# A 3x3 convolution of image rows in blocks of four from six (six products in place of twelve), inside a kernel with attention and dynamic filters

## The chip, the cores and the metric

One core of one Trainium2 chip. The time is device microseconds (us) of one execution, the median of several. "Ratio" is the mean time of one kernel's fast runs over the mean of the other kernel's fast runs in the same rounds, with a 95% interval; it is therefore not quite the ratio of the medians quoted beside it. Runs of different calls are compared through their ratios to the kernel before, which ran again in each call (medians 3262.8 to 3268.4 us).

Engines: PE is TensorE's matrix multiplication, PEld its weight load, DVE VectorE, ACT ScalarE, POOL GpSimd, SP the queue that issues most transfers.

## The reference, cut to what matters

```python
# x: 4 images, 256 channels, 48 x 48, fp32
x = x + layer0(group_norm(x))   # conv 3x3, batch norm, relu, qkv 1x1, attention (8 heads), projection
x = x + layer1(group_norm(x))   # below

def layer1(x):
    guidance = conv3x3(x, W_cat)                     # 45 maps = 5 dilations x 9 taps
    outs = [x]
    for i, d in enumerate((1, 6, 12, 24, 36)):
        w = softmax(guidance[:, 9*i:9*(i+1)], axis=1)
        outs.append(sum of 9 shifted copies of x, each times one map of w)   # "dynamic filter"
    y = conv1x1(concat(outs), W_scale)               # 1536 -> 256 channels, "the mix"
    return batch_norm_with_batch_statistics(y)       # over all four images
```

## The kernel before: the parts that matter

Image 0's convolution runs alone. Then attention of image b alternates with a *mixed stage*, in which the dynamic filters of image b and the convolution and qkv of image b+1 share the engines. There are three mixed stages, then a last filter stage without a convolution, then a tail that reloads, normalizes and stores everything.

```python
# the convolution: 6 row blocks x 2 output halves x 18 matmuls of 384 columns an image, straight from the padded image
nc.tensor.matmul(pc[:, :CH], wc[:, i, k, o * P : (o + 1) * P],
                 window(gn, i, c * R, k // 3 - 1, k % 3 - 1), ...)
...                                    # ScalarE: relu(scale * pc + bias) -> hid
# one tap of a dynamic filter
nc.tensor.matmul(pw[:, : nr * WW], pick[:, k : k + 1].to_broadcast([2 * NG, P]), w[...])  # "wb": a map on 128 partitions
nc.vector.tensor_tensor(pv, wb, src, ALU.mult)        # "prod": PSUM x SBUF, five buffers
dst = accv[:, :, l0:l1, x0:x1]
eng = nc.vector if n in own else nc.gpsimd            # own = {1} in the last stage, else empty
eng.tensor_tensor(dst, dst, pv, ALU.add)              # "cat": four buffers
tap += 1
owed += NH * nr * ncol * rate
pump()                                                # issue the other work's matmuls for that much TensorE time
```

`pump` hands out matmuls of three queues: mixes of finished accumulators, the guidance of later rows, and the next image's convolution and qkv. So the convolution is filler for TensorE between the taps. The filter's two sides are: TensorE (wb) to VectorE (prod) to GpSimd (add) to TensorE (mix).

## Time and profile before

| | before |
|---|---|
| time, median | 3268.6 us |
| first convolution matmul; start of attention of image 0 | 19.95; 209.2 us |
| mixed stage 2: lead-in, filter stretch | 64.7, 293.5 us |
| GpSimd busy in that stretch | 258.8 us (88%) |
| tail: from the last copy of a result out of PSUM to the end | 42.8 us |

Read it by stage, not by totals. The *lead-in* of a mixed stage is from attention's end to GpSimd's first add, the *filter stretch* from there to its last add. The prediction shows these rows for the first mixed stage. The second one is the same to 0.1 us. Columns: stretch, its length, then busy time (instructions) of PE, PEld, DVE, ACT and POOL, the granted TensorE clock, the DMA engines' share and GB/s.

```profile
1374.30:1439.00 64.70, 64.70 (x248) 34.92 (x246) 14.47 (x31) 5.83 (x10) 0.00 (x0) 0.97 0.05 13
1439.00:1732.50 293.50, 293.50 (x1102) 184.15 (x1101) 198.24 (x287) 33.24 (x56) 258.78 (x192) 1.00 0.05 14
```

TensorE is full in both; GpSimd is close behind in the second.

### The profile page before, as it was taken

Reading aid. Unit: us, or ns where it says so; the run is one execution under the profiler, and the core shown is the slowest. Engines: PE = TensorE matmul, PEld = TensorE weight load, DVE = VectorE, ACT = ScalarE, POOL = GpSimd, SP = SyncE. Lnnn points to the kernel's source line nnn. Section 1 sums busy time; section 2 is a strip of 40 time slices with the busy share of each in tenths; the row PEclk is TensorE's granted clock in tenths of the full one; section 3 lists DMA queues with packets and bytes.
Section 4 is the critical chain, followed back from the end, with each engine's and each line's share of the span. In section 5 each row is a group of like instructions: output and inputs, shape, how many; then the busy total and the mean of one; then the engine's idle time right before and its main releaser. Section 6 shows DMA issues by size and latency. Waiting matters only on the chain.

```text
span 3262.5 us, 43612 instructions
## 1 busy us (share of the span) xinstructions
PE 3099.3 (95%) x18070; PEld 1390.5 (43%) x18070; DVE 2272.3 (70%) x2149; ACT 1491.8 (46%) x1673; POOL 973.3 (30%) x746
## 2 busy tenths in 40 slices
PE   7999999999999999999999999999999999978883
PEld 4542223555662222456664222355565222234442
DVE  2048888556668888736676888836666898867776
ACT  0058887400028887600026887820013888740002
POOL 0000000069870000038982000008885000006663
PEclk9999999999999999999999999999999999988876
DMA  3020000000003000000003000000001000031004
GB/s 124 15 44 6 4 3 11 16 15 20 10 13 56 6 6 11 11 8 25 13 10 63 6 6 11 6 6 5 10 5 39 1 5 6 11 140 49 10 5 184
DMA packets 71245, 81.40 MB, mean 25 GB/s; under 512 B 51568, under 2 KB 62336, under 8 KB 67968
## 3 DMA queue, kind: packets, MB, share of 16 engines
q1 hardware_dynamic: 70240, 73.15, 8.0%
q0 software_dynamic: 800, 5.41, 0.4%
q8 instruction: 142, 2.33, 0.3%
q14 instruction: 63, 0.52, 0.1%
HBM read 50.23 MB, written 28.31 MB: 24 GB/s over the span
## 4 chain that ended last, share of the span: by engine, by line
PE 87%; DVE 5%; ACT 4%; issue 2%; DMA 1%; POOL 0%; SPq 0%; DVEq 0%; ACTq 0%; POOLq 0%
PE se L718 20%; PE pc L637 17%; PE num L748 17%; PE py L1008 12%; PE wb L1067 5%; PE pg L890 5%; PE pq L660 4%; PE den L770 3%; ACT p L727 3%; PE pp L819 2%; DVE acc L763 2%; PE pv L679 2%; DVE prod L1088 1%; ACT no L766 1%; POOL cat L1091 0%
## 5 line engine op out<-in xcount | busy, mean ns | idle before, releaser
L1091 POOL TENSOR_TENSOR cat<-cat,prod 128x752 f32<-128x752 f32 (+8 forms) x720 | 965.9, 1349 | 2240.4 <-DVE prod L1088 1261.4
L727 ACT ACTIVATE p<-se 128x1024 f32<-128x1024 f32 x1296 | 1259.2, 1026 | 277.5 <-PE se L718 238.3
L763 DVE TENSOR_TENSOR acc<-acc,p 128x2048 f32<-128x2048 f32 x504 | 1154.6, 2291 | 108.5 <-ACT p L727 69.6
L718 PE MATMUL se<-q,k 32*128 32x512 f32 (+1 forms) x5760 | 802.6, 592 | 11.2 <-ACT p L727 8.0
L1088 DVE TENSOR_TENSOR prod<-wb,pad 128x768 f32<-128x768 f32 (+7 forms) x768 | 558.9, 748 | 269.2 <-PE wb L1067 260.8
L748 PE MATMUL num<-p,vT 128*32 128x512 f32 (+1 forms) x5760 | 694.0, 561 | 8.8 <-ACT no L766 7.4
L637 PE MATMUL pc<-pad,wc 128*128 128x384 f32 x1728 | 611.6, 490 | 2.3 <-issue 2.3
L1067 PE MATMUL wb<-w,pick 90*128 90x384 f32 (+3 forms) x888 | 470.9, 558 | 51.7 <-DVE prod L1088 43.8
L718 PEld LDWEIGHTS se<-q,k 32*128 32x128 f32 x5760 | 291.3, 183 | 526.6 <-issue 422.2
L637 PEld LDWEIGHTS pc<-pad,wc 128*128 128x128 f32 x1728 | 322.4, 191 | 192.5 <-issue 12.7
L1008 PE MATMUL py<-cat,wsc 128*128 128x384 f32 x960 | 365.8, 514 | 0.5 <-POOL cat L1091 0.5
L748 PEld LDWEIGHTS num<-p,vT 128*32 128x32 f32 x5760 | 121.6, 108 | 486.7 <-issue 438.4
L1067 PEld LDWEIGHTS wb<-w,pick 90*128 90x128 f32 x888 | 172.3, 196 | 202.9 <-DVE prod L1088 76.0
L646 ACT ACTIVATE hid<-pc,bn_t_f,bn_s_f 128x384 f32<-128x384 f32 x48 | 32.2, 671 | 460.9 <-PE pc L637 460.9
L1008 PEld LDWEIGHTS py<-cat,wsc 128*128 128x128 f32 x960 | 189.4, 202 | 106.0 <-issue 18.5
L1082 DVE TENSOR_TENSOR cat<-wb,pad 128x768 f32<-128x768 f32 x114 | 108.5, 952 | 90.3 <-PE wb L1067 90.3
L890 PE MATMUL pg<-pad,wcat 128*45 128x384 f32 x864 | 153.5, 498 | 2.6 <-DVE pad L587 2.4
L1023 ACT COPY y<-py 128x768 f32<-128x768 f32 x24 | 19.2, 799 | 277.1 <-PE py L1008 277.1
L660 PE MATMUL pq<-hid,wqkv 128*128 128x384 f32 x384 | 135.3, 485 | 0.0
L763 DVE TENSOR_TENSOR acc<-p,p 128x2048 f32<-128x2048 f32 x36 | 82.5, 2293 | 66.1 <-ACT p L727 66.1
L670 DVE TENSOR_REDUCE qkpart<-q 128x1 f32<-128x384 f32 x48 | 26.5, 552 | 140.7 <-ACT q L667 139.1
L660 PEld LDWEIGHTS pq<-hid,wqkv 128*128 128x128 f32 x384 | 71.4, 190 | 41.2
(124 smaller groups left out, 1175.3 us busy)
## 6 DMA issues: line engine op xcount, KB each, us to landing
pad<-in_x SPq DMA_DIRECT2D x14, 1152.0 KB, 14.8
x_d<-pad SPq DMA_DIRECT2D x48, 192.0 KB, 2.5
y_d<-y SPq DMA_DIRECT2D x24, 384.0 KB, 2.7
xst<-in_x SPq DMA_DIRECT2D x36, 192.0 KB, 2.4
y<-y_d SPq DMA_DIRECT2D x3, 2304.0 KB, 19.6
out<-y SPq DMA_DIRECT2D x6, 1152.0 KB, 12.4
x<-x_d SPq DMA_DIRECT2D x2, 2304.0 KB, 24.4
x_first<-in_x SPq DMA_DIRECT2D x2, 1152.0 KB, 7.3
```

What stands on the lines that cost most here:

```text
L637: nc.tensor.matmul(pc[:, :CH], wc[:, i, k, o * P : (o + 1) * P], window(gn, i, c * R, k // 3 - 1, k % 3 - 1), start=(i == 0 and k == 0), s ...
L660: nc.tensor.matmul(pq[:, :CH], wqkv[:, i, s, g * P : (g + 1) * P], hid[:, i, cols], start=(i == 0), stop=(i == NH - 1),)
L718: nc.tensor.matmul(ss[j // 2][:, j % 2, at : at + n], k_[r, g, m * P : (m + 1) * P], q[r, g, q0 : q0 + n], start=True, stop=True,)
L727: nc.scalar.activation(p[:, 2 * pair : 2 * pair + 2, :], ss[pair], AF.Exp, scale=QS)
L748: nc.tensor.matmul(st["num"][r, at : at + n], vT[:, m, g * P + j * D : g * P + (j + 1) * D], p[:, j, at : at + n], start=(m == 0 and not s ...
L763: nc.vector.tensor_tensor(st["acc"], other, p, ALU.add)
L890: nc.tensor.matmul(pg[64 * s : 64 * s + NG, :CH], wcat[:, i, k, :], window(gn, i, (c + s) * R, k // 3 - 1, k % 3 - 1), start=(i == 0 and k ...
L1008: nc.tensor.matmul(py[c][:, o, :CH], wsc[:, n * NH + i, o * P : (o + 1) * P], rhs(i), start=(n == 0 and i == 0), stop=(last and i == NH - 1),)
L1067: nc.tensor.matmul(pw[:, : nr * WW], pick[:, k : k + 1].to_broadcast([2 * NG, P]), w[:, l0 * WW : l1 * WW], start=True, stop=True,)
L1082: nc.vector.tensor_tensor(accv, wb, src, ALU.mult)
L1088: nc.vector.tensor_tensor(pv, wb, src, ALU.mult)
L1091: eng.tensor_tensor(dst, dst, pv, ALU.add)
```

## The change

Intent: compute four output rows from six input rows (a minimal-filtering scheme along y), so that per four rows there are six products of three column taps in place of twelve: half of the multiplications. In exchange the inputs (VectorE), the weights (GpSimd and ScalarE, once, stored to DRAM and reloaded for later images) and the outputs (VectorE) are transformed on the chip.

```diff
-        wc = wpool.tile([P, NH, 9, C], F32, tag="wc", name="wc")
...                                     # (the weights now live in a pool of image 0 only)
+        def made_from(wc, pool):       # weights of product i, image 0
+            def make(i):
+                if i == 1: eng.tensor_tensor(t, w[0], w[2], ALU.add)          # eng = GpSimd, 1536 elements
+                if i in (1, 3): eng.tensor_tensor(u, t, w[1], ALU.add)
+                if i in (2, 4): eng.tensor_tensor(u, t, w[1], ALU.subtract)
...                                     # i = 3: two more and a nc.scalar.mul; i = 0, 5: nc.scalar.mul
+                nc.sync.dma_start(out=u_d[i], in_=u)
+        def inputs(stage, g):          # VectorE, three rounds, g = upper or lower half
+            if stage == 0:   4 x axpy of 300 elements; 2 x tensor_tensor of 600
+            elif stage == 1: 4 operations of 600, two SBUF inputs each
+            else:            4 operations of 600, two SBUF inputs each
+        def outputs(i, g, o, m):       # VectorE, m = the product in PSUM, 288 elements
...
+            elif i == 0:
+                result(1, d34, -2.0, d12)
+                result(2, s34, -4.0, s12)
+                tt(s12, s12, s34, ALU.subtract)
+                axpy(d12, d34, -8.0, d12)
+                result(0, m, None, s12)
...
+            for at, i in enumerate(ORDER):      # 6 products x 2 halves x 2 output blocks x 6 matmuls of 288
+                    if at == 0: inputs(0, g)
+                    if at in (1, 3): inputs((at + 1) // 2, g)
...
-            t = [last.tile(...) for j in range(2)]
+            t = [last.tile(...) for j in range(3)]     # tail: image 2's result is reloaded here
+            nc.sync.dma_start(out=t[2], in_=y_d[B - 2])
```

(Bodies shortened; the lines of `outputs` are whole.) The first four lines under `i == 0` (the "combinations") take both operands from SBUF; the fifth reads the product in PSUM.

More of the change, by code (lines that the diff above doesn't have):

```diff
@@ L523, in conv_preact_kernel @@
     y_d = tc.dram_tile([B, P, NH, N], F32, name="y_d")
+    u_d = tc.dram_tile([6, P, NH, 3, C], F32, name="u_d")
     with tc.tile_pool(name="w", bufs=1) as wpool, tc.tile_pool(
@@ L544, in conv_preact_kernel @@
         wsc = wpool.tile([P, (1 + len(DILATIONS)) * NH, C], F32, tag="wsc", name="wsc")
-        for h in range(NH):
-            nc.gpsimd.dma_start(out=wc[:, h], in_=conv_w[:, h])
-        nc.gpsimd.dma_start(out=wqkv, in_=qkv_w)
-        nc.gpsimd.dma_start(out=wp, in_=proj_w)
-        nc.gpsimd.dma_start(out=vbc, in_=v_b.rearrange("(h p) -> p h", p=P))
-        nc.gpsimd.dma_start(out=wcat, in_=cat_w)
-        nc.gpsimd.dma_start(out=wsc, in_=scale_w)
         ones = wpool.tile([P, D], F32, tag="ones", name="ones")
@@ L560, in conv_preact_kernel @@
         )
-        lgs = [wpool.tile([P, CH], F32, tag=f"lg{j}", name=f"lg{j}") for j in range(2)]
-        for lg in lgs:
-            nc.gpsimd.memset(lg, 0.0)
+        lg = wpool.tile([P, CH], F32, tag="lg", name="lg")
+        nc.gpsimd.memset(lg, 0.0)
         yst = wpool.tile([P, NH, B * NCK, 6], F32, tag="yst", name="yst")
         bn_s, bn_t = conv_norm(wpool, "f")
+        bn_s6 = wpool.tile([P, NH], F32, tag="bn_s6", name="bn_s6")
+        nc.vector.tensor_scalar(bn_s6, bn_s, -1.0 / 6.0, None, ALU.mult)
         pads = []
@@ L627, in conv_preact_kernel @@
         MM = 27.0 / 16 * CH
-        def conv_qkv(b, gn, psum_tile, q, k_, vT, after):
-            hid = keep("h", f"hid_{b}")
-            for c in range(NCK):
-                for o in range(NH):
-                    pc = psum_tile(f"pc_{b}_{c}_{o}")
-                    for i in range(NH):
-                        for k in range(9):
-                            nc.tensor.matmul(
-                                pc[:, :CH],
-                                wc[:, i, k, o * P : (o + 1) * P],
-                                window(gn, i, c * R, k // 3 - 1, k % 3 - 1),
-                                start=(i == 0 and k == 0),
-                                stop=(i == NH - 1 and k == 8),
-                            )
-                            if k < 8 or i < NH - 1:
-                                yield MM
-                    nc.scalar.activation(
-                        hid[:, o, c * CH : (c + 1) * CH], pc[:, :CH], AF.Relu,
-                        bias=bn_t[:, o : o + 1], scale=bn_s[:, o : o + 1],
-                    )
-                    yield MM
+        ORDER = (1, 2, 3, 4, 0, 5)
@@ new lines, in conv_preact_kernel, with taken_from, load @@
+        TJ = HH // 4 // 2
+        TN = TJ * WW
+        def taken_from(pool):
+            def load(i):
+                u = pool.tile([P, NH, 3, C], F32, tag="u", name=f"u_{i}")
+                nc.sync.dma_start(out=u, in_=u_d[i])
+                return u
+            return load
+        def made_from(wc, pool):
+            w = [wc[:, :, 3 * j : 3 * j + 3, :] for j in range(3)]
+            t = pool.tile([P, NH, 3, C], F32, tag="ut", name="u_t")
+            def make(i):
+                u = pool.tile([P, NH, 3, C], F32, tag="u", name=f"u_{i}")
+                eng = nc.gpsimd
+                if i == 1:
+                    eng.tensor_tensor(t, w[0], w[2], ALU.add)
+                if i == 3:
+                    eng.tensor_scalar(t, w[0], 0.25, None, ALU.mult)
+                    eng.tensor_tensor(t, t, w[2], ALU.add)
+                    nc.scalar.mul(w[1], w[1], 0.5)
+                if i in (1, 3):
+                    eng.tensor_tensor(u, t, w[1], ALU.add)
+                if i in (2, 4):
+                    eng.tensor_tensor(u, t, w[1], ALU.subtract)
+                if i == 0:
+                    nc.scalar.mul(u, w[0], -1.5)
+                if i == 5:
+                    nc.scalar.mul(u, w[2], -6.0)
+                nc.sync.dma_start(out=u_d[i], in_=u)
+                return u
+            return make
@@ new lines, in conv, with axpy, relu, result @@
+        def conv(b, gn, psum_tile, weights, pool, hid):
+            halves = [
+                act.tile([P, NH, 6, TJ, PADW], F32, tag=tag, name=f"cv_{b}_{tag}")
+                for tag in ("q", "k")
+            ]
+            held = act.tile([P, 4, 2 * NH, TN], F32, tag="v", name=f"cs_{b}")
+            S12, D12, S34, D34 = range(4)
+            place = {1: 1, 2: 2, 3: 3, 4: 4, 0: 1, 5: 2}
+            def inputs(stage, g):
+                v = [halves[g][:, :, i].rearrange("p h t w -> p h (t w)") for i in range(6)]
+                v4 = [halves[g][:, :, i] for i in range(6)]
+                d = [
+                    gn[:, :, 4 * TJ * g + r : 4 * TJ * g + r + 4 * TJ - 3 : 4, :] for r in range(6)
+                ]
+                tt, stt = nc.vector.tensor_tensor, nc.vector.scalar_tensor_tensor
+                def axpy(out, x, a, y):
+                    stt(out=out, in0=x, scalar=a, in1=y, op0=ALU.mult, op1=ALU.add)
+                if stage == 0:
+                    for h in range(NH):
+                        axpy(v4[5][:, h], d[2][:, h], -4.0, d[4][:, h])
+                        axpy(v4[0][:, h], d[1][:, h], -4.0, d[3][:, h])
+                    tt(v[1], v[5], v[0], ALU.add)
+                    tt(v[2], v[5], v[0], ALU.subtract)
+                elif stage == 1:
+                    tt(v4[5], d[4], d[2], ALU.subtract)
+                    tt(v4[0], d[3], d[1], ALU.subtract)
+                    axpy(v[3], v[0], 2.0, v[5])
+                    axpy(v[4], v[0], -2.0, v[5])
+                else:
+                    tt(v4[1], d[0], d[2], ALU.subtract)
+                    axpy(v[1], v[1], 4.0, v[5])
+                    tt(v4[2], d[5], d[3], ALU.subtract)
+                    axpy(v[2], v[0], -4.0, v[2])
+            def relu(g, o, r, y):
+                rows = hid.rearrange("p h (t r w) -> p h t r w", r=4, w=WW)
+                nc.scalar.activation(
+                    rows[:, o, TJ * g : TJ * g + TJ, r, :], rows_of(y), AF.Relu,
+                    bias=bn_t[:, o : o + 1], scale=bn_s6[:, o : o + 1],
+                )
+            first = {}
+            def outputs(i, g, o, m):
+                at = NH * g + o
+                s12, d12, s34, d34 = (held[:, j, at] for j in range(4))
+                tt, stt = nc.vector.tensor_tensor, nc.vector.scalar_tensor_tensor
+                def axpy(out, x, a, y):
+                    stt(out=out, in0=x, scalar=a, in1=y, op0=ALU.mult, op1=ALU.add)
+                def result(r, x, a, y):
+                    t = pool.tile([P, TN], F32, tag="yt", name=f"yt_{b}_{g}_{o}_{r}")
+                    if a is None:
+                        tt(t, x, y, ALU.add)
+                    else:
+                        axpy(t, x, a, y)
+                    relu(g, o, r, t)
+                if i in (1, 3):
+                    first[at] = pool.tile([P, TN], F32, tag="m1", name=f"m_{b}_{i}_{at}", bufs=4)
+                    nc.scalar.copy(first[at], m)
+                elif i == 2:
+                    tt(s12, m, first[at], ALU.add)
+                    tt(d12, first[at], m, ALU.subtract)
+                elif i == 4:
+                    tt(s34, m, first[at], ALU.add)
+                    tt(d34, first[at], m, ALU.subtract)
+                elif i == 0:
[4 more added lines that the diff above has]
+                    result(0, m, None, s12)
+                else:
+                    result(3, m, None, d12)
+            ahead = weights(ORDER[0])
+            for at, i in enumerate(ORDER):
+                u = ahead
+                if at + 1 < len(ORDER):
+                    ahead = weights(ORDER[at + 1])
+                for g in range(2):
+                    if at == 0:
+                        inputs(0, g)
+                    if at in (1, 3):
+                        inputs((at + 1) // 2, g)
+                    for o in range(NH):
+                        pc = psum_tile(f"pc_{b}_{i}_{g}_{o}")
+                        m = pc[:, :TN]
+                        for h in range(NH):
+                            for kx in range(3):
+                                nc.tensor.matmul(
+                                    m,
+                                    u[:, h, kx, o * P : (o + 1) * P],
+                                    halves[g][:, h, place[i], :, kx : kx + WW],
+                                    start=(h == 0 and kx == 0),
+                                    stop=(h == NH - 1 and kx == 2),
+                                )
+                                if h < NH - 1 or kx < 2:
+                                    yield MM * TN / CH
+                        outputs(i, g, o, m)
+                        yield MM * TN / CH
@@ L652, in conv_qkv @@
+        def conv_qkv(b, gn, psum_tile, weights, pool):
+            hid = keep("h", f"hid_{b}")
+            yield from conv(b, gn, psum_tile, weights, pool, hid)
+            q, k_ = keep("q", f"q_{b}"), keep("k", f"k_{b}")
+            vT = act.tile([P, NT, C], F32, tag="v", name=f"vT_{b}")
+            qkv[b] = q, k_, vT
             part = small.tile([P, 2, NH, NCK], F32, tag="qkpart", name=f"qkpart_{b}")
@@ L694, in conv_qkv @@
             nc.vector.tensor_copy(bound[:, b, :], pb[:, :NH])
-            after()
-        CONV_QKV = MM * (NCK * NH * (18 + 4) + NT * 2 * C / CH)
+        qkv = {}
+        CONV_QKV = MM * (6 * 4 * 6 * TN / CH + NCK * NH * 4 + NT * 2 * C / CH)
         def attention(b, q, k_, vT, pools, spare, project):
@@ L898, in weights @@
                             yield 3 * MM
-                lg = lgs[(c // 2) % 2]
                 for s in range(2):
@@ L1033, in dynamic_filters @@
                     for bb, (ty, tx) in enumerate(again):
-                        nc.sync.dma_start(out=ty[:, :, :N], in_=y_d[bb])
+                        if ty is not None:
+                            nc.sync.dma_start(out=ty[:, :, :N], in_=y_d[bb])
                         nc.sync.dma_start(out=tx[:, :, :N], in_=x1_d[bb])
@@ L1174, in conv_preact_kernel @@
                                       norm0.rstd, h)
-                    q, k_ = keep("q", f"q_{b}"), keep("k", f"k_{b}")
-                    vT = act.tile([P, NT, C], F32, tag="v", name=f"vT_{b}")
+                    weights = taken_from(work1)
+                    if b == 0:
+                        wc = work1.tile([P, NH, 9, C], F32, tag="wc", name="wc", bufs=1)
+                        for h in range(NH):
+                            nc.gpsimd.dma_start(out=wc[:, h], in_=conv_w[:, h])
+                        nc.gpsimd.dma_start(out=wqkv, in_=qkv_w)
+                        nc.gpsimd.dma_start(out=wp, in_=proj_w)
+                        nc.gpsimd.dma_start(out=vbc, in_=v_b.rearrange("(h p) -> p h", p=P))
+                        nc.gpsimd.dma_start(out=wcat, in_=cat_w)
+                        nc.gpsimd.dma_start(out=wsc, in_=scale_w)
+                        weights = made_from(wc, work1)
                     nn, stats = None, iter(())
@@ L1181, in conv_preact_kernel @@
                     other = merged(
-                        conv_qkv(b, pads[b % 2], psc, q, k_, vT, lambda: None), 40000.0, 6000.0,
+                        conv_qkv(b, pads[b % 2], psc, weights, work1), 40000.0, 4000.0,
                         stats,
@@ L1201, in conv_preact_kernel @@
                             (act.tile([P, NH, N], F32, tag="v", name="y_1"), pad_0),
-                            (wpool.tile([P, NH, N], F32, tag="wc", name="y_2"), keep("h", "x1_2")),
+                            (None, keep("h", "x1_2")),
                         ]
@@ L1237, in conv_preact_kernel @@
             norm1 = Norm("n1", b)
+            q, k_, vT = qkv[b]
             with tc.tile_pool(name=f"work0_{b}", bufs=2) as work0, tc.tile_pool(
@@ L1248, in conv_preact_kernel @@
         with tc.tile_pool(name="last", bufs=1) as last:
-            t = [last.tile([P, NH, N], F32, tag=f"last{j}", name=f"last{j}") for j in range(2)]
+            t = [last.tile([P, NH, N], F32, tag=f"last{j}", name=f"last{j}") for j in range(3)]
+            nc.sync.dma_start(out=t[2], in_=y_d[B - 2])
+            again[B - 2] = t[2], again[B - 2][1]
             for o in range(NH):
@@ L1252, in conv_preact_kernel @@
                 nc.sync.dma_start(out=t[1][:, o], in_=x1_d[B - 1, :, o])
-            again.append(tuple(t))
+            again.append(tuple(t[:2]))
             for b in range(B):
```

## The prediction

> **What bounds the kernel now.** I read the page's busy line first, then its 40 slices, then the busy time of each engine by stage, because the 70% of VectorE and 30% of GpSimd are averages over stages with different limits.
>
> ```profile
> span 3262.5 us, 43612 instructions
> PE 3099.3 (95%) x18070; PEld 1390.5 (43%) x18070; DVE 2272.3 (70%) x2149; ACT 1491.8 (46%) x1673; POOL 973.3 (30%) x746
> ...
> PE   7999999999999999999999999999999999978883
> POOL 0000000069870000038982000008885000006663
> PEclk9999999999999999999999999999999999988876
> ```
>
> The digits show one lone convolution (image 0), then attention alternating with a mixed stage in which GpSimd works: there the dynamic filters of image b-1 and the convolution of image b share the engines (about 610 to 975, 1374 to 1740 and 2139 to 2504 us). The last GpSimd stretch has no convolution. Busy time by stretch (PE, weight loads, VectorE, ScalarE, GpSimd, granted clock):
>
> ```profile
> 20.00:161.00 141.00, 141.00 (x433) 82.54 (x434) 7.76 (x13) 7.41 (x12) 0.00 (x0) 1.00 0.10 28
> 161.00:209.00 48.00, 47.60 (x178) 32.89 (x176) 14.04 (x29) 19.88 (x34) 0.00 (x0) 1.00 0.45 81
> 609.80:674.50 64.70, 64.70 (x250) 35.11 (x246) 14.48 (x31) 5.83 (x10) 0.00 (x0) 0.97 0.05 13
> 674.50:968.00 293.50, 293.50 (x1102) 184.17 (x1102) 198.24 (x287) 33.23 (x56) 258.73 (x192) 1.00 0.05 14
> 968.00:975.20 7.20, 6.27 (x26) 3.69 (x25) 0.22 (x2) 1.39 (x2) 0.00 (x0) 1.00 0.00 0
> 2960.00:3220.00 260.00, 206.66 (x567) 113.68 (x565) 194.97 (x278) 13.45 (x21) 173.81 (x134) 0.79 0.02 8
> 3220.00:3262.00 42.00, 0.20 (x2) 0.11 (x2) 23.28 (x21) 18.93 (x10) 0.00 (x0) 0.51 0.86 348
> ```
>
> To be seen: conv 0 is pure TensorE. In a mixed stage TensorE is full for 64.7 us before GpSimd has anything (the lead-in), and for the 293.5 us in which GpSimd adds its products; but GpSimd is itself 258.7 of those 293.5 us busy, 88%. That second, hidden bound decides this prediction. The tail is DMA (0.86 of the engines).
>
> The chain of waits gives the price of a convolution, and the waits of 690 to 975 us show that VectorE, and through it GpSimd, waits for TensorE there:
>
> ```profile
> 19.95 140.99 PE pc L637 x432
> ...
> 191.90 15.54 PE pv L679 x72
> ```
>
> ```profile
> DVE prod L1088 <- PE wb L1067: 62.1, 97, 1.7
> ...
> POOL cat L1091 <- DVE prod L1088: 23.3, 26, 2.0
> ```
>
> **What the Trainium skill says.** (1) "VectorE: DVE Perf Modes", section on the TRN2 errata: an fp32 tensor_tensor takes (N+151)/0.96 ns. The trace agrees: 2048 elements give 2291 ns against 2290.6. So I price 288 elements at 457, 300 at 470, 600 at 782 ns. (2) "GPSIMD Engine Reference", section on elementwise cycle accounting: about 2.6 cycles an element. The adds of 768 and 384 elements take 1821 and 1000 ns: 2.14 ns an element, 2.56 cycles, plus 180 ns. 1536 elements: 3.46 us. (3) "SBUF — State Buffer", "Who interferes with whom": a VectorE instruction with two SBUF inputs and a GpSimd instruction that reads SBUF exclude each other for the whole instruction. The trace agrees on VectorE's side: the same subtraction of 270 elements takes 0.44 us at 648.02 with GpSimd idle and 1.18 us at 805.36 with it busy. Today's products read one operand from PSUM and are free of this; most of the new transforms are not. (4) "TensorE: Matmul & The Clock Gate", on the clock gate: the clock halves after an idle window of about 3.4 us. The last stage, TensorE 79% busy in records, shows 0.79 granted.
>
> **The change part by part.**
>
> *TensorE.* A matmul leaves two records. Today 12 row blocks x 18 = 216 matmuls an image of 384 columns; 140.99/432 = 326 ns a record, 0.85 ns a column. The change issues 6 products x 4 groups x 6 = 144 of 288 columns. 256 columns cost 15.54/72 = 216 ns a record, so the price stays 0.85 ns a column and weight loads (189 ns) stay hidden: 288 x 0.85 = 244 ns, x288 = 70.3 us. Each image loses 70.7 us of TensorE, four images 283 us. That is the ceiling.
>
> *Conv 0.* Alone, so its TensorE time counts. But its start is later: the weight DMA is queued on GpSimd behind the memsets (roughly +3 us; before, issue at 2.1 us plus 10.9 to land, so I take 15 to 16 us), then two GpSimd adds of 1536 elements (6.9 us) to about 22.5. The normalized image is ready at 21.2; VectorE's first transforms follow, 4 x 0.47 + 2 x 0.78 = 3.4 us, delayed by the exclusion against GpSimd's adds. First matmul at about 28 instead of 19.95: I choose +8. Later weights need one add (3.46 us) after a buffer comes free, inside a product of 24 x 0.488 = 11.7 us: hidden. I allow 2 us of stalls, since the two PSUM buffers are now emptied partly by VectorE. Net: 70.7 - 8 - 2 = 60 us saved.
>
> *Lead-in of a mixed stage.* The old convolution could start at once from the padded image. The new one waits until VectorE has closed attention (last multiply done at 612.5) and made transforms (3.4 us): first matmul at about 616 in place of 609.8, on a cooled clock. The second half's transforms come before the filter's statistics on the same queue: about 4 us more. Against that, the fixed amounts of convolution used as filler are rounded to smaller matmuls: 67 x 0.652 = 43.7 us becomes 75 x 0.488 = 36.6, saving 7. Walking the order through to the first filter matmul I get it at 674.8 instead of 670.5: +4.3 us. Lead-in 69.
>
> *The filter stretch.* TensorE's need: 67 of 216 matmuls ran in the lead-in, so 149 x 0.652 = 97 us are here now, and (144-75) x 0.488 = 34 afterwards: 293.5 - 63 = 230 us. GpSimd's need stays 258.7, so GpSimd becomes the bound. Its idle time, now 35 us, shrinks because VectorE no longer waits on TensorE; starts of accumulators and small edge taps keep some: I choose 10. VectorE gains here about 4 transforms of 782 ns, 16 combinations of 457 ns with two SBUF inputs (10.5 us, which exclude GpSimd, so about +10 for it) and some 12 of 288 elements from PSUM (5 us): 198 + 16 and waits for the lock, under 80% of the stretch. Sum: 258.7 + 10 + 10 = 279, against 293.5.
>
> A mixed stage: 69 + 279 + 7.2 = 355 against 365.4, 10 to 11 us saved, three times: 32. So 60 of each stage's 71 us on TensorE turn into idle time there.
>
> *Weights.* Six loads of 768 KB an image, one product ahead; the DMA engines are 5% busy. Nothing.
>
> *Tail.* The array for one image's result was the old weight tile; now 2.36 MB of image 2 is reloaded after the last store. The tail moved 348 GB/s x 42 us; 2.36 MB at that rate is 6.8 us: +7.
>
> *Attention, qkv, last filter stage*: same instructions; nothing.
>
> Sum: -60 - 32 + 7 = -85: 3268.6 - 85 = about **3183 us**. I round to 3182.
>
> **The rivals.**
> *A: TensorE remains the bound everywhere.* Then 283 - 10 - 7 is gained: about 3000. For it: TensorE is 100% busy in mixed stages today. Against: GpSimd's 258.7 us cannot shrink; even with no gap a stage is 65 + 259 + 7 = 331, so no less than 3268 - 60 - 103 + 7 = 3112 can come out.
> *B: GpSimd is fed without gaps and the lock costs little.* Idle 5, lock 3: a stage of 343, 22 saved each: about 3148. For it: five product buffers, VectorE at under 80%, and the transforms come in blocks of four or five behind such a backlog.
> *C: the mixed stages slow down in new ways.* TensorE at some 82% loses its full clock as in the last stage, VectorE's blocks of transforms (each op waiting for a GpSimd add, 1.4 us on average) drain the backlog. Then a mixed stage saves nothing: about 3215. For it: the last stage, where no engine is over 80% busy and GpSimd only 67%. Against: TensorE's real work there is far thinner than 82%.
>
> **Range and chances.** The certain part is conv 0 minus the tail, -53, 1.6%. The 2% line is at 3203; it needs only 4 us from each mixed stage. B and my own sum are beyond it, C is not. I give 3145 to 3214 for 8 in 10, and 0.77 faster, 0.21 within 2%, 0.02 slower.
>
> **What would show each step.** Per-record matmul time of the new convolution in stage 0: 244 ns. First convolution matmul near 28 us and attention near 149 instead of 209. In mixed stages: first GpSimd add some 4 us later after attention's end than 64.8, GpSimd over 90% busy from there to its end, TensorE near 82%, and the waits turned round: VectorE's products waiting for GpSimd, no longer for TensorE. Transforms with two SBUF inputs well over 457 ns there. Tail 49 us. I am wrong if mixed stages fall below 340 (lock and gaps overrated) or stay at 365 (clock under 0.95 in them, or GpSimd idle over 30 us).

## The result, and the profile after

3209.6 us median (3209.4 to 3210.2, four runs) against 3268.4 us: ratio 0.9824, interval 0.9807 to 0.9841. So the change gained 1.8%, inside the range but 28 us short of the predicted 3182, and on the other side of the 2% line than the likelier call.

Page of the changed kernel: span, busy time, 40 slices.

```profile
span 3208.1 us, 42897 instructions
...
PE 2892.8 (90%) x17494; PEld 1301.4 (41%) x17494; DVE 2441.5 (76%) x2422; ACT 1514.4 (47%) x1724; POOL 1005.5 (31%) x752
...
PE   5999999979899999898999999987989999978873
...
POOL 4000000189940000058980000018894000007672
PEclk9999999999999999999999999999999999988876
```

TensorE lost 206 us of busy time, the span 54 us: most of what was saved on TensorE became idle time there, in the mixed stages, where its digits fall to 7 and 8. By stretch (lead-in, filter stretch, its two parts, the end piece up to the next attention, and the tail):

```profile
1321.00:1391.90 70.90, 60.65 (x272) 39.27 (x266) 32.16 (x64) 8.18 (x16) 0.00 (x0) 0.90 0.20 67
1391.90:1681.10 289.20, 256.63 (x954) 161.90 (x950) 219.94 (x324) 37.31 (x64) 260.80 (x192) 0.95 0.05 17
1391.90:1500.00 108.10, 90.49 (x350) 55.63 (x347) 89.55 (x126) 10.53 (x18) 90.32 (x67) 0.94 0.06 19
1500.00:1681.10 181.10, 166.15 (x608) 106.27 (x605) 130.38 (x199) 26.78 (x46) 170.47 (x125) 0.96 0.05 16
1681.10:1685.20 4.10, 3.17 (x12) 1.53 (x10) 0.03 (x1) 0.80 (x1) 0.00 (x0) 1.00 0.00 0
3157.00:3208.10 51.10, 0.20 (x2) 0.11 (x2) 23.60 (x21) 19.41 (x11) 0.00 (x0) 0.52 0.82 333
```

(The first window opens 0.9 us before the end of attention's sums; the lead-in itself is 70.1 us.) GpSimd is now busy 90% of the stretch: 84% of its first 108 us, in which the convolution's transforms still run, and 94% of the rest. The waits turned round in part. In the later part of the stretch (engine, line, tile it waited with, releaser: us, times, longest), before:

```profile
DVE prod L1088 <- PE wb L1067: 40.3, 60, 1.6
```

and after:

```profile
DVE prod L1222 <- POOL cat L1225: 19.0, 25, 1.8
DVE prod L1222 <- PE wb L1201: 15.4, 17, 2.1
```

So VectorE now also waits for a product buffer that GpSimd has yet to free, where it used to wait for TensorE alone; but waits for TensorE remain. In the whole stretch they went from 68.0 to 27.9 us, and those for GpSimd from 1.1 to 20.9. The start of the program, on VectorE of the changed kernel (start, us, engine, line, operation; in brackets idle time before it):

```profile
15.49 2.36 DVE L609 TENSOR_TENSOR gd_n<-mvn,gmean_n 128x2 f32<-128x2 f32 x1
...
18.08 3.27 DVE L611 TENSOR_TENSOR gd_n<-gd_n,mvn 128x2 f32<-128x2 f32 x1
...
22.66 2.06 DVE L618 SCALAR_TENSOR_TENSOR gshift_n<-gmean_n,grstd_n 128x2 f32<-128x2 f32 x1
24.64 6.64 DVE L582 TENSOR_SCALAR pad<-x_first,gmean_n,grstd_n 128x2304 f32<-128x2304 f32 x2
31.20 4.82 DVE L690 SCALAR_TENSOR_TENSOR cv_q<-pad 128x300 f32<-128x300 f32 x4
```

and on GpSimd:

```profile
14.41 3.42 POOL L653 TENSOR_TENSOR u_t<-wc 128x1536 f32<-128x1536 f32 x1 [6.34 <-DMA wc<-in_conv_w]
17.91 3.42 POOL L659 TENSOR_TENSOR u<-u_t,wc 128x1536 f32<-128x1536 f32 x1
21.29 3.41 POOL L661 TENSOR_TENSOR u<-u_t,wc 128x1536 f32<-128x1536 f32 x1
24.80 5.26 POOL L655 TENSOR_SCALAR u_t<-wc 128x1536 f32<-128x1536 f32 x1
```

An operation on two elements takes 2 to 3.3 us, and each of them ends just where a GpSimd instruction ends (17.9, 21.3, 24.8 us). In the kernel before, where GpSimd has no instruction at that time, the same three took 0.16 us each and the normalization 2.87. The chain into the first convolution matmul runs through exactly these, and that matmul comes at 36.98 us.

Where the 54.4 us of span come from:

| part | predicted | measured in the trace |
|---|---|---|
| start of attention of image 0 | -60 | -50.9 (209.2 to 158.3) |
| from there to the start of attention of image 3 (three mixed stages) | -32 | -5.8 (766.0, 764.5, 764.7 to 762.6, 764.3, 762.5) |
| last attention, last filter stage and tail | +7 | +2.3 (tail alone 42.8 to 51.0) |
| sum | -85 | -54.4 |

### The profile page after: what moved, and what is told of

Same layout as the page of the kernel before. It is cut to its first block, busy times and chain, and to the rows that moved or that the text cites. A ratio compares the mean times of both kernels' runs of the same rounds, so it can differ in the third digit from the quotient of the medians.

```text
span 3208.1 us, 42897 instructions
## 1 busy us (share of the span) xinstructions
PE 2892.8 (90%) x17494; PEld 1301.4 (41%) x17494; DVE 2441.5 (76%) x2422; ACT 1514.4 (47%) x1724; POOL 1005.5 (31%) x752
## 4 chain that ended last, share of the span: by engine, by line
PE 72%; DVE 12%; POOL 6%; ACT 4%; issue 4%; DMA 2%; SPq 0%; DVEq 0%; POOLq 0%; ACTq 0%
PE se L852 21%; PE num L882 18%; PE py L1141 10%; PE pc L766 7%; POOL cat L1225 6%; PE pg L1024 5%; DVE prod L1222 4%; PE wb L1201 3%; PE den L904 3%; ACT p L861 3%; PE pq L794 2%; PE pp L953 2%; DVE acc L897 2%; PE pv L813 1%; DVE yt L723 1%
## 5 line engine op out<-in xcount | busy, mean ns | idle before, releaser
L1222 DVE TENSOR_TENSOR prod<-wb,pad 128x768 f32<-128x768 f32 (+7 forms) x768 | 551.6, 746 | 203.7 <-PE wb L1201 135.7
L1201 PE MATMUL wb<-w,pick 90*128 90x384 f32 (+3 forms) x888 | 434.4, 530 | 98.1 <-DVE prod L1222 86.8
L1141 PE MATMUL py<-cat,wsc 128*128 128x384 f32 x960 | 397.0, 543 | 43.0 <-POOL cat L1225 43.0
L1141 PEld LDWEIGHTS py<-cat,wsc 128*128 128x128 f32 x960 | 197.5, 212 | 152.0 <-POOL cat L1225 52.6
L766 PE MATMUL pc<-cv_q,u 128*128 128x288 f32 x576 | 165.1, 426 | 36.8 <-DMA u<-u_d 21.8
L766 PE MATMUL pc<-cv_k,u 128*128 128x288 f32 x576 | 164.0, 422 | 8.8 <-DVE cv_k L695 8.7
L766 PEld LDWEIGHTS pc<-cv_q,u 128*128 128x128 f32 x576 | 112.5, 201 | 69.9 <-issue 41.3
L766 PEld LDWEIGHTS pc<-cv_k,u 128*128 128x128 f32 x576 | 110.3, 197 | 37.9 <-issue 10.0
L710 ACT ACTIVATE hid<-yt,bn_t_f,bn_s 128x288 f32<-128x288 f32 x64 | 39.7, 626 | 167.7 <-DVE yt L728 97.7
```

Of the source, the lines that this page charges most:

```text
L766: nc.tensor.matmul(m, u[:, h, kx, o * P : (o + 1) * P], halves[g][:, h, place[i], :, kx : kx + WW], start=(h == 0 and kx == 0), stop=(h == ...
L1141: nc.tensor.matmul(py[c][:, o, :CH], wsc[:, n * NH + i, o * P : (o + 1) * P], rhs(i), start=(n == 0 and i == 0), stop=(last and i == NH - 1),)
```

## The experiments

Theory 1 is the prediction's: after the change GpSimd bounds the filter stretch and TensorE's freed time is idle. Theory 2: VectorE, with the transforms, bounds it. Theory 3: TensorE still does, at a lower clock. The length of the filter stretch in the three stages is what to compare (before 293.4, 293.3, 293.4 us; after 289.8, 289.1, 287.1 us).

**1. GpSimd's adds of one dilation left out, in the changed kernel.** The result is wrong.

```diff
-                        eng.tensor_tensor(dst, dst, pv, ALU.add)
+                        if not (b < B - 1 and n == 2):
+                            eng.tensor_tensor(dst, dst, pv, ALU.add)
```

> The changed kernel, but GpSimd leaves out its adds for dilation 12 in the three mixed stages (a wrong result on purpose). Those are 42 adds and 24192 elements a stage: 24192 x 2.14 ns + 42 x 0.18 us = 59 of its 261 us. Theory 1 (GpSimd is the bound of the mixed stages after the change, and the TensorE time that the change freed lies idle): GpSimd falls to about 202 us, TensorE's own need of 231 to 243 us becomes the bound, so each filter stretch goes from 289 to 245 to 258 us; 95 to 130 us in all, 3080 to 3115 us. Theory 2 (VectorE, with its transforms, is the bound): VectorE still makes every product, so under 10 us a stage, over 3180 us. Theory 3 (TensorE at its lowered clock of 0.95 still is the bound): no change either.

Measured: 3156.7 us, ratio 0.9672. The second mixed stage's stretch, and its later part:

```profile
1373.60:1641.80 268.20, 245.64 (x945) 156.22 (x940) 214.18 (x323) 36.67 (x63) 201.11 (x150) 0.97 0.06 18
1480.00:1641.80 161.80, 153.69 (x584) 99.98 (x584) 126.63 (x196) 26.24 (x45) 126.26 (x95) 0.99 0.06 18
```

The stretches are 271.8, 268.1 and 270.5 us: 17 to 21 us shorter, where theory 1 expected 31 to 44, theory 2 under 10 and theory 3 nothing. So theories 2 and 3 fall, and GpSimd was a bound, but it lies only some 20 us above the next one. In the later part TensorE takes over (95% busy, clock 0.99). In the first 106 us no engine is full: GpSimd 70%, VectorE 82%, TensorE 86%. Theory 1 as I had stated it, one bound at a time, is too simple there.

**2. The same in the kernel before.** Same edit.

> The same adds left out of the kernel before (wrong result on purpose). If TensorE alone bounds its mixed stages, as the prediction has it, nothing happens: within 8 us of the kernel before, GpSimd falling from 259 to about 200 us a stretch of still 293. If GpSimd had already been a bound of its own beside TensorE, some 10 us or more a stage, 3240 us or less.

Measured: 3266.4 us, ratio 1.0004 (0.9987 to 1.0020).

```profile
1438.20:1731.50 293.30, 293.30 (x1102) 184.13 (x1101) 197.48 (x287) 33.23 (x56) 199.91 (x150) 1.00 0.05 14
```

Removing 59 us of GpSimd work moves the stretch by 0.2 us: TensorE was the only bound. The same edit is worth nothing before the change and 1.5% after it (0.9824 to 0.9672). The bound did change hands.

**3. TensorE's work given back.** Every convolution matmul of images 1 to 3 is issued twice (wrong result; start and stop flags and the pacing's total adapted).

```diff
+                        reps = 2 if b else 1
                         for h in range(NH):
                             for kx in range(3):
-                                nc.tensor.matmul(
...
+                                for rep in range(reps):
+                                    nc.tensor.matmul(
...
```

> The changed kernel with every convolution matmul of images 1 to 3 issued twice (wrong result on purpose; the pacing of the filler told of it): 70 us more of TensorE work a mixed stage, about what the change took away. Theory 1: the stretch only has to hold 231 + 70 = 301 us of TensorE work where it takes 289 now, so 12 to 20 us a stage, 3245 to 3270 us, GpSimd back to some 86% of the stretch. If TensorE were still the bound (theory 3), all 70 us would show: about 3410 us. If instead the low clock of 0.95 were what costs, the fuller TensorE would get its clock back and the stage would lengthen by less than 10 us.

Measured: 3298.7 us, ratio 1.0106.

```profile
1425.00:1735.70 310.70, 302.32 (x1228) 207.73 (x1225) 227.41 (x331) 38.70 (x67) 260.70 (x192) 1.00 0.06 21
```

Of the 70 us added a stage some 30 show (89 us in all by the medians), 40 are absorbed: theory 3, which wanted all 70, falls, and so does its other form, that only the clock cost time. The clock did return to 1.00 and the stage still grew. But I had expected 12 to 20 us a stage. The stretch, 310.7 us, is about 3% over the 301 us of work, and the lead-in grew too. TensorE's room is thus about 40 us a stage, not the 58 that its need on paper (231 of 289 us) suggests.

**4. Most transforms left out** for images 1 to 3: rounds two and three of the inputs and the four combinations of two SBUF operands (wrong result).

```diff
-                    if at in (1, 3):
+                    if at in (1, 3) and b == 0:
                         inputs((at + 1) // 2, g)
...
-                    result(1, d34, -2.0, d12)
-                    result(2, s34, -4.0, s12)
-                    tt(s12, s12, s34, ALU.subtract)
-                    axpy(d12, d34, -8.0, d12)
+                    if b:                            # images 1 to 3
+                        relu(g, o, 1, d12)
+                        relu(g, o, 2, s12)
...                                                      # else: the four combinations
```

> The changed kernel without VectorE's second and third round of input transforms and without its four combinations of two SBUF inputs per group in images 1 to 3 (wrong result on purpose, the matmuls and GpSimd's adds unchanged). Theory 1: GpSimd keeps its 261 us and its own small gaps; only the part of its idle time that follows transform blocks goes, 10 to 15 us a stage: 3163 to 3180 us. Theory 2 (the transforms are what ate the gain): the stretch falls to the 270 us floor or under it, 19 us or more a stage: 3150 us or less.

Measured: 3166.4 us, ratio 0.9701.

```profile
1378.50:1654.40 275.90, 251.53 (x954) 159.77 (x949) 200.53 (x304) 36.41 (x64) 258.22 (x192) 0.96 0.05 18
```

The stretches are 276.2, 275.8 and 272.2 us, 13 to 15 us shorter. GpSimd is busy 258.2 us, 94% of the stretch, which is as good as its later part in the changed kernel. So 13.3 us of the second stage's stretch are the transforms' and 17.7 us of idle time would be there without them. Most of the 17.7 us can be read on GpSimd itself. A group of adds in the changed kernel's timeline that is nowhere broken by a wait:

```profile
1500.04 43.37 POOL L1225 TENSOR_TENSOR cat<-cat,prod 128x752 f32<-128x752 f32 x29 [0.40 <-DVE prod L1222]
```

and the busy time of that stretch:

```profile
1500.04:1543.41 43.37, 39.48 (x165) 23.07 (x161) 31.09 (x46) 3.32 (x6) 41.72 (x29) 0.96 0.06 19
```

29 adds one after another occupy 43.37 us but count as 41.72 us busy: 57 ns on average between two, waiting for nothing. At that mean the 192 adds of a stretch have 10.9 us of such spaces (an estimate), which no better feeding would remove.

**5. Do GpSimd's long instructions hold VectorE at the start?** The weight transforms of image 0 in six instructions of 256 elements each (same result).

```diff
+                def each(f):
+                    for h in range(NH):
+                        for kx in range(3):
+                            f(lambda a: a[:, h, kx, :])
-                    eng.tensor_tensor(t, w[0], w[2], ALU.add)
+                    each(lambda s: eng.tensor_tensor(s(t), s(w[0]), s(w[2]), ALU.add))
...                                                   # the other five alike
```

> The changed kernel with GpSimd's weight transforms for image 0 cut into six instructions of 256 elements each instead of one of 1536 (same result). If VectorE's small operations and its normalization wait at the start because GpSimd holds SBUF for a whole instruction (3.4 to 5.3 us), each wait shrinks to under 1 us: the normalized image is ready about 4 us earlier and the first convolution matmul comes at 31 to 34 us instead of 37.0; 3 to 6 us in all, although GpSimd's own work grows from 6.9 to 8.7 us for the first weights (6 x 0.73 us twice, from the 0.18 us per instruction and 2.14 ns per element of the trace before). If the start is late for another reason (the weights themselves, their DMA), it comes at 37 or later.

Measured: 3201.0 us, ratio 0.9801, correct. The operations shown above, in this run:

```profile
15.61 0.65 DVE L609 TENSOR_TENSOR gd_n<-mvn,gmean_n 128x2 f32<-128x2 f32 x1
...
16.97 0.65 DVE L611 TENSOR_TENSOR gd_n<-gd_n,mvn 128x2 f32<-128x2 f32 x1
...
18.93 0.73 DVE L618 SCALAR_TENSOR_TENSOR gshift_n<-gmean_n,grstd_n 128x2 f32<-128x2 f32 x1
19.58 3.75 DVE L582 TENSOR_SCALAR pad<-x_first,gmean_n,grstd_n 128x2304 f32<-128x2304 f32 x2
```

Operations of 2 to 3.3 us become 0.65 to 0.73, the normalization takes 3.75 us in place of 6.64, the first convolution matmul comes at 28.34 us and attention at 149.7, better than I expected of the run and just what the prediction had for the change itself (28 and 149). So the start was late because VectorE was held for as long as a whole long GpSimd instruction ran. About 3.5 of these 8.6 us were lost again before GpSimd's first add, in the first attention, whose clock was 0.97 in its first 100 us where the changed kernel has 1.00. That is one trace, and I did not test it.

**6. The start repaired in another way**: image 0 normalized on ScalarE, and the weight stores issued by the engines that made them (same result).

```diff
-                            normalize(inside(pads[0], h), rows_of(x_first[:, h, :]), ...)
+                            nc.scalar.activation(inside(pads[0], h), rows_of(x_first[:, h, :]), AF.Identity,
+                                bias=norm0.shift[:, h : h + 1], scale=norm0.rstd[:, h : h + 1])
...
-                nc.sync.dma_start(out=u_d[i], in_=u)
+                (nc.scalar if i in (0, 5) else nc.gpsimd).dma_start(out=u_d[i], in_=u)
```

> The changed kernel with image 0 normalized on ScalarE[...], and with the stores of the transformed weights issued from the queues of the engines that made them, so that the loads of image 1's rows are no longer queued behind them (same result). The small VectorE operations still wait for GpSimd. Expected: first convolution matmul at 31 to 34 us instead of 37.0, the gap of 3 to 4 us of TensorE near 92 us gone; 7 to 10 us in all, 3200 to 3203 us.

Measured: 3208.2 us (3204.0 to 3213.4), ratio 0.9830 (0.9813 to 0.9846): in time no different from the changed kernel, although the profiled run (span 3202.2 us) has its first convolution matmul at 32.25 us and attention at 152.55, 5.8 us earlier. The second half of my expectation was a misreading: VectorE does wait 2.8 us there for a row of image 1 behind a weight store, but the 24 matmul records of that group take 6.19 us in place of 5.82, so TensorE lost 0.4 us and not 3 to 4. The run is inconclusive as to the time.

**7. Blocks or exclusion?** The transforms issued one at a time between matmuls, in place of blocks of four (same operations, same result).

```diff
                         for h in range(NH):
                             for kx in range(3):
                                 nc.tensor.matmul(m, u[:, h, kx, ...], ...)
+                                if i == 0 or kx % 2 == 0:
+                                    next(side, None)      # one operation of inputs() or outputs()
                                 if h < NH - 1 or kx < 2:
                                     yield MM * TN / CH
```

> The changed kernel with the transforms of the second and third round and the four combinations issued one at a time between the matmuls of the running product instead of in blocks of four (same operations, same result). If the 13 to 14 us that the transforms cost a stage come from blocks that hold VectorE for 4 to 5 us while GpSimd runs dry, most of it comes back: 8 to 13 us a stage, 3170 to 3185 us. If they come from the exclusion itself (each operation with two SBUF inputs keeps GpSimd out for as long as it runs), whether in a block or alone, it is under 3 us a stage: over 3200 us.

Measured: 3201.4 us, ratio 0.9805. The stretches are 286.3, 286.3 and 286.4 us, 0.8 to 3.5 us shorter than after. Of the 13 us a block of operations explains the smaller part, about 2.

**8. Work moved from GpSimd to TensorE**: in each row block of the mixed stages one full product goes straight into the mix (four more matmuls) instead of through a GpSimd add.

```diff
+                        if direct:                        # one tap of dilation 1 per row block
+                            for o in range(NH):
+                                queue.append((tap + 4, mix(c, n + 1, o, lambda i, prod=prod: prod[:, i, :])))
+                        else:
                             eng.tensor_tensor(dst, dst, pv, ALU.add)
```

(One buffer of its own for such products, paid for with one of the two buffers of the stored result.)

> The changed kernel, but in the mixed stages one full product of each row block goes straight to TensorE's mix (four more matmuls of 0.648 us) instead of through a GpSimd add of 1.82 us (same result up to rounding). Theory 1 (GpSimd bounds, TensorE has idle time): GpSimd 261 to 250 us, TensorE's need 231 to 247 us, the stretch 8 to 12 us shorter, 3170 to 3185 us. Theory 3 (TensorE, at its lower clock, bounds): 15 us a stage longer, about 3255 us. Theory 2 (VectorE bounds): within 3 us a stage.

Measured: 3213.3 us, ratio 0.9842 (0.9826 to 0.9859): no gain. A miss for theory 1 in its simple form. The stretches did shrink, to 287.7, 285.1 and 284.8 us, by 2 to 4 where I expected 8 to 12. What was won in the second was given back around it: from attention's start to the first add 1.7 us more, and the end piece 7.1 in place of 4.1 us, for TensorE had its other work still to do when GpSimd was done. The stages are so near a balance of three coupled engines that 12 us less on one and 15.6 more on another come out even.

**9. The exclusion alone.** For images 1 to 3 each combination reads the product's PSUM tile in place of its second SBUF operand: same number, size and place of instructions, wrong values.

```diff
+                    f, e = (m, m) if b else (d34, s34)
-                    result(1, d34, -2.0, d12)
-                    result(2, s34, -4.0, s12)
-                    tt(s12, s12, s34, ALU.subtract)
-                    axpy(d12, d34, -8.0, d12)
+                    result(1, f, -2.0, d12)
+                    result(2, e, -4.0, s12)
+                    tt(s12, e, s12, ALU.subtract)
+                    axpy(d12, f, -8.0, d12)
```

> The changed kernel in which, for images 1 to 3, each of the four output combinations per group reads one operand from the product's PSUM tile in place of the second operand in SBUF (wrong result on purpose; same count, size and place of instructions, same time that the PSUM tile is held). If the exclusion between VectorE's instructions with two SBUF inputs and GpSimd is what the transforms cost (13 us a stage when they are all left out; these 12 to 16 of 457 ns are 5.5 to 7.3 of the 10.7 us of such operations in the filter stretch), 5 to 10 us a stage come back although VectorE's queue is as long as before, and the operations take about 450 ns in place of 1045 to 1300: 3180 to 3195 us. If VectorE's time or order is what costs, whatever the operands, under 2 us a stage: over 3202 us.

Measured: 11960.6 us, which says nothing. The program checks a bound on attention's scores at its end and, where that is too large, computes everything again in a slow, safe way; the wrong values tripped it. I had not thought of that. But the fast path ran first, whole, and the trace shows its stages. The combinations in the changed kernel, second stretch (count, busy us, mean ns):

```profile
L723 DVE SCALAR_TENSOR_TENSOR yt<-cs 128x288 f32<-128x288 f32 x8 | 10.1, 1300 | 0.0
...
L745 DVE TENSOR_TENSOR cs<-cs 128x288 f32<-128x288 f32 x4 | 4.2, 1045 | 0.1
```

and in this run:

```profile
L723 DVE SCALAR_TENSOR_TENSOR yt<-pc,cs 128x288 f32<-128x288 f32 x8 | 3.2, 444 | 0.0
...
L746 DVE TENSOR_TENSOR cs<-pc,cs 128x288 f32<-128x288 f32 x4 | 1.8, 457 | 0.1
```

with the stretch

```profile
1385.50:1666.10 280.60, 251.92 (x954) 158.43 (x949) 211.15 (x324) 36.93 (x64) 259.79 (x192) 0.97 0.05 17
```

The stretches are 280.5, 280.6 and 281.1 us: 9.3, 8.5 and 6.0 us shorter with the same queue of instructions, where leaving most transforms out gave 13.6, 13.3 and 14.9. So the exclusion on the combinations alone makes up about two thirds of the cost in the first two stages and 40% in the third. The traces show how it works here: an operation with two SBUF operands waits for GpSimd's add to end, and while VectorE waits it makes no products, so GpSimd runs dry. (The last combination of a block, a `cs<-cs` on L723 that comes when GpSimd has run dry, took only 449 ns in the changed kernel.) That GpSimd is itself kept out by a running operation shows little: its busy time is 260.8 us with the transforms and 258.2 without them.

**10. Deeper buffers**: five accumulators in place of four, mixes queued nine taps after the last product in place of six (and one buffer of the stored result in place of two).

```diff
-CATS = 4
+CATS = 5
-                                    tap + PRODS + 1,
+                                    tap + PRODS + 4,
```

> The changed kernel with five accumulator buffers in place of four (the third buffer of the stored result given up for space) and TensorE's mixes queued nine taps after an accumulator's last product in place of six (same result). If the coupling of in-order engines through few buffers is what keeps GpSimd from its floor (TensorE waits 12 to 14 us a stage for GpSimd's accumulators, and VectorE and GpSimd behind it), 3 to 6 us a stage come back: 3190 to 3200 us. If GpSimd's own adds and the exclusion are the whole bound, within 1 us a stage: 3205 to 3212 us.

Measured: 3200.3 us, ratio 0.9795, at the edge of the first range, but not for its reason: the stretches are 290.0, 289.2 and 288.2 us, unchanged or longer. What is gained lies in the last stage: from the last add of the third mixed stage to the start of the last copy of a result 705.4 us in place of 712.6. In the mixed stages of the changed kernel, buffers alone were not the limit.

**11. Four repairs together**: 5, 6 and 7, and the tail's reload of image 2 moved into the last filter stage, where it fits into the space that the convolution's buffers leave.

```diff
+            if b == B:
+                y2 = late.enter_context(tc.tile_pool(name="late", bufs=1)).tile([P, NH, N], F32, ...)
-                            (None, keep("h", "x1_2")),
+                            (y2, keep("h", "x1_2")),
```

> The changed kernel with four repairs together (same result): weight transforms of image 0 in small pieces, its normalization on ScalarE and its weight stores off the loads' queue, the transforms spread one at a time, and image 2's result reloaded during the last filter stage into space that the convolution's buffers leave free there. From the single runs: 7 us for the pieces, about 3 more for the rest of the start, 6 for the spreading, and the 8 us by which the tail grew: 3208 - 24 = 3184 us, ratio to the kernel before 0.973 to 0.978. If the start repairs all shorten the same wait, 3 less; if the reload only moves the 2.36 MB to where it disturbs the filter stage, 8 less, 3192 us.

Measured: 3187.3 us, ratio 0.9757 (0.9744 to 0.9770), correct. Attention of image 0 starts at 151.1 us, the stretches are 286.1, 286.1 and 286.4 us, and the tail is 45.1 us in place of 51.0. The last filter stage is no longer for the reload in it: from attention of image 3 to the start of the last copy it takes 705.9 us, where the changed kernel took 708.6.

**12. These four and the deeper buffers.**

> The four repairs together and the deeper buffers of the run before (five accumulators, mixes queued nine taps later; same result). The trace of the deeper buffers gave nothing in the mixed stages and 7.2 us in the last filter stage, which none of the four repairs touches: 3187 - 7 = 3180 us, ratio 0.972 to 0.975. If that gain of the last filter stage is taken by the reload of image 2's result, which now runs there, nothing: 3187 us.

Measured: **3174.4 us, ratio 0.9719** (0.9706 to 0.9733), correct: 2.8% under the kernel before and about 1% under the change. Second mixed stage:

```profile
1379.10:1660.10 281.00, 251.74 (x954) 156.57 (x949) 224.12 (x326) 37.56 (x64) 262.12 (x192) 0.98 0.05 17
```

More than the sum, and for a reason that the single runs did not show: the stretches are now 281.0, 280.9 and 279.4 us, 8 us shorter than after, though spreading alone gave about 2 and the buffers alone nothing there. Neither the blocks nor the accumulators alone set the pace; with both eased GpSimd is 93% busy over the whole stretch. That both are needed is measured; which wait stands behind which, I did not trace.

## Why the prediction was right or wrong

*TensorE's price.* Right. 24 records of the new convolution take 5.82 us, 242 ns each (predicted 244), and image 0's convolution takes 72.9 us from its first matmul (70.3 and up to 2 for stalls were predicted).

*Conv 0.* The term of its start was mis-sized: +17.0 us (19.95 to 36.98) where the prediction chose +8. I had priced the weights' own chain and named the exclusion only for the transforms. The trace shows it earlier: on the two-element operations of the group norm (2.36 + 3.27 + 2.06 = 7.7 us, before 0.16 each) and on the normalization (6.64 us, before 2.87), which has only one tensor as input, so that the prediction's "two SBUF inputs" did not cover it. Experiment 5 shows the cause: with shorter GpSimd instructions the first matmul comes at 28.3 us, as predicted.

*Lead-in.* +5.4 us measured in the second stage (64.7 to 70.1 from the end of attention's sums), +4.3 predicted. Right in kind and nearly in size. But the prediction's "Nothing" for the weights was a little wrong. In each mixed stage the first convolution matmul waits 7.3 us, last for the reload of its weights, which is issued only at attention's end (1324.71 us, in the second stage):

```profile
1329.20 3.22 PE L766 MATMUL pc<-cv_q,u 128*128 128x288 f32 x6 [7.34 <-DMA u<-u_d]
```

The transforms were done at 1327.6, so the weights cost 1.6 us there. An earlier reload was not tried.

*Filter stretch.* This is the step that failed in size. "258.7 + 10 + 10 = 279" was 289.2 us. The mechanism held in its main point: experiments 1 and 2 show that GpSimd's adds were worth nothing before, with TensorE busy all the time, and 17 to 21 us a stretch after. It was too simple in another: "VectorE no longer waits on TensorE" failed, for 27.9 of 68.0 us of these waits remained, and TensorE was busy 89% of the stretch, not 82%. The term for idle time was 17.7 us in place of 10 (experiment 4, without the transforms), of which some 10.9 us are the spaces of 57 ns between adjacent adds; I had taken a GpSimd instruction's recorded time for all that it occupies. The term for the transforms was 13.3 us in place of 10 (258.2 + 17.7 + 13.3 = 289.2); experiment 9 attributes 8.5 of them to the exclusion, experiment 7 about 2 to their coming in blocks; the rest I did not take apart. And TensorE's room was smaller than its need of 230 us said: it absorbs about 40 us, not 60 (experiment 3). So GpSimd is not the bound alone: 59 us less for it gave only 17 to 21 (experiment 1).

*Rival C.* "A mixed stage saves nothing" was closer than my own sum. Its second reason, VectorE's blocks waiting for GpSimd's adds, is much of what happened. Its first, the lost clock, was not the main one (0.95 was granted, and experiments 4 and 9 took 13.3 and 8.5 us off the stretch at 0.96 and 0.97); what the clock alone cost was not tested. On the rule of the clock in the prediction's point (4) the trace agrees: after those 7.3 us without a matmul 0.50 was granted from 1328 to 1332 us, and 1.00 again from 1336 to 1340. By its own sign of being wrong ("stay at 365", "GpSimd idle over 30 us") the prediction came close to failing: the second mixed stage takes 363.3 us, with GpSimd idle for 28.4 of its stretch.

*Around the stretch.* The end piece fell from 7.2 to 4.1 us. Of attention I wrote "nothing"; the one before the second stage takes 401.0 us in place of 399.2. From the start of that attention to the start of the next, all parts together come out even: +5.4 - 4.3 - 3.1 + 1.8 = -0.2.

*Tail.* +8.2 us (+7 predicted), right. Attention of image 3 and the last filter stage up to the start of the last copy, for which I predicted no change, took 708.6 us in place of 714.6. I first put that down to the reload that moved from there to the tail, but in experiment 11 the reload is back and the stage is as short (705.9 us); so the cause of these 6 us stays open.

*The sum.* -54.4 in the trace, -85 predicted: 9 us are the start, 26 the three mixed stages, and 5 of the other sign the last stage. The range held because it was drawn down to rival C, not because the sum was good.

## What to carry to other kernels

When a change takes a large part of one engine's work away, look at once for the engine that is nearly full beside it (88% here), and price its floor with the gaps between its instructions, not by its busy time. Work that is moved from TensorE to VectorE beside a busy GpSimd is charged twice if its operands are both in SBUF: VectorE waits for GpSimd's instruction to end, and GpSimd then waits for VectorE; cut the long instruction or let one operand come from PSUM. In a balanced chain of engines, as here, repairs made singly can show nothing and together give their gain.

## What the Trainium skill lacked or had wrong

- "GPSIMD Engine Reference" (section 3.1) prices an instruction by itself and names its dispatch without a figure. "Perfetto Trace Analysis" (section "GPSIMD Engine Instruction") does advise to time GpSimd from start to start. Both lack the size of the space between two: 57 ns on average between adjacent adds that wait for nothing (29 adds, 41.72 us busy in 43.37), some 4% of this stage's GpSimd time.
- "SBUF — State Buffer" (section "Who interferes with whom") states the exclusion as the runs show it on VectorE's side. What it lacks is the size of it for small operations: two-element VectorE operations took 0.16 us with GpSimd idle, 2.06 to 3.27 us beside GpSimd instructions of 3.4 us, and 0.65 to 0.73 us when those were cut into six.
- No page read has a way to price engines that are coupled through few buffers: here 59 us less of GpSimd work gave 17 to 21 us a stretch, and 70 us more of TensorE work cost some 30 us a stage.
